# Two graph layers on one core: loads and stores by column of row blocks in place of by partition block, and another order in the front

## The chip, the cores and the metric

One Trainium2 chip, one core of it. The time is that of the device for the whole kernel, in microseconds; the median over runs is compared. A profiled execution gives the trace.

## The reference

32 graphs (batches) of 512 nodes with 512 features each, all float32, through two layers:

```
# layer 0
h   = relu(layernorm(x))
agg = (adj @ h) / max(rowsum(adj), 1e-6)
x   = x + relu(concat(h, agg) @ W.T)               # W: 512 x 1024
# layer 1
h   = relu(layernorm(x))
q, k = split(h @ Wqk);  v = h @ Wv
w   = mask * rowdot(q, adj @ (k * mask)) / sqrt(512)
x   = x + softmax(w over nodes)[:, None] * v
```

## The kernel before

Every 512 x 512 x 512 product is done in float32 on TensorE by a scheme of seven half-size products in place of eight (the tiles named pp, pq, pr hold its sums in PSUM; left and right sums of quadrants are made on DVE). Layer 0 is Y = h W2^T, then o = h W1^T + A Y with A the row-normalized adjacency; layer 1 uses M = Wq Wk^T and computes t = h1 M and v = h1 Wv together (`layer1_tv`, tiles ptv, line 470), u = A (mask h1), and the score as the row product of t and u. So a batch costs TensorE four phases: `layer0_y`, `layer0_out`, `layer1_tv`, `layer1_u`.

A tile of 512 rows holds row q\*128 + c\*32 + r in partition q\*32 + r, column c (q, c from 0 to 3, r from 0 to 31). DVE turns 32 x 32 blocks, so a transposed matrix is made by writing the rows to a scratch in DRAM (dhT, daT, dh1T), reading it back with an exchange of blocks (`exchange`, line 206: four DMAs, one for each q) and turning it on DVE.

The order of all engines is written by hand (`manual_schedule`): each phase is a generator of products, and a `Plan` says after which product the other work is issued. All loads and stores of the steady state are issued on SP's queue, in this order of the program; an issue that has to wait for a semaphore holds everything behind it. x1 is added to the result by an accumulating DMA from POOL (`add_x1`).

The lines that the change and the prediction touch:

- `by_rows` (188), `load_rows` (193), `half_rows` (202): loads of x (tile xu, by `load_x`), of x again for the next batch's layer 0 (tile n, `FrontH.load`), of adj (tile a, `FrontA.load`), and of Wv. Each DMA takes one q: 32 partitions, with 4 columns (256 KB) or 2 (128 KB).
- `store` (714) and, for the last batch, `store_block` (708): the result to DRAM, likewise one DMA for each q.
- w<-dw (line 415): W1's seven slots are streamed from a scratch in DRAM, 256 KB a slot, 128 partitions a DMA, seven per batch.
- `start` (778), the front: it loads Wk in two halves and Wq in four pieces of rows, turns them on DVE, and multiplies them to M on TensorE (`multiply`, line 839) while x[0] arrives, is normalized, and turned through TensorE (h). ACT issues half of these DMAs and does nothing else until its table load at the first copy. Before the data is there, TensorE runs five products of zeros (spare, line 819).

Of the kernel before, what the change touches and what calls it, by code (L numbers as in the profile page):

```python
# [22 lines left out]
def kernel(  # L23
# [11 lines left out]
    nc = tc.nc  # L35
    B, N, F = x.shape
    C = N // P
    H = F // 2
    Q = 4
    R = 32  # L40
# [26 lines left out]
    def mm_tile(name):  # L67
        return ps_m.tile([P, 2, H], F32, tag="m", name=name)
# [10 lines left out]
    def copy(o, i):  # L79
        nc.scalar.activation(o, i, AF.Copy)  # L80
# [104 lines left out]
        def at(self, n, f, *args):  # L185
            self.setdefault(n, []).append(lambda: f(*args))

    def by_rows(src):

        t = src.rearrange("(q c r) f -> q r c f", q=Q, c=C)  # L190
        return [t[q] for q in range(Q)]

    def load_rows(t, src):
        for q, rows in enumerate(by_rows(src)):
            nc.sync.dma_start(out=t[q * R:(q + 1) * R, :, :], in_=rows)

    def half_tile(name):
        return big.tile([P, 2, 512], F32, tag="n", bufs=2, name=name)
# [1 line left out]
    one_queue, two_queues = (nc.sync, nc.sync), (nc.sync, nc.scalar)  # L200

    def half_rows(t, src, h, queues=one_queue):
        for q, rows in enumerate(by_rows(src)):
            queues[q % 2].dma_start(out=t[q * R:(q + 1) * R, :, :], in_=rows[:, 2 * h:2 * h + 2, :])

    def exchange(src, name, t=None, queues=one_queue):


        if t is None:
            t = big.tile([P, 8, P], F32, tag="s", bufs=2, name=name)  # L210
        for q in range(Q):
            queues[q % 2].dma_start(
                out=t[q * R:(q + 1) * R, :, :], in_=src[:, :, ts(q, P)].rearrange("k r j -> r k j")
            )
        return t


    mhalf = const.tile([P, C], F32, name="mhalf")
    nc.vector.memset(mhalf, -0.5)

    X, AT_, DEG, W, Y, H1M, H1T, U, TV, HT = ({} for _ in range(10))

    def xu_tile(name):
        return big.tile([P, C * 512], F32, tag="xu", bufs=2, name=name)

    def room_x(b):

        t = xu_tile(f"xu_{b}")
        X[b] = t.rearrange("p (c f) -> p c f", c=C)
        U[b] = t.rearrange("p (k i f) -> p k i f", k=4, i=2)  # L230

    def load_x(b):
        room_x(b)
        load_rows(X[b], x[b])

    def norm_tiles(name):
        k = name[0]
        mv = small.tile([P, C, 2], F32, tag=f"mv{k}", name=f"mv{name}")
        rstd = small.tile([P, C], F32, tag=f"rstd{k}", name=f"rstd{name}")
        nmr = small.tile([P, C], F32, tag=f"nmr{k}", name=f"nmr{name}")  # L240
        return mv, rstd, nmr

    def statistics(src, t, c, name):
        st = small.tile([P, 6], F32, tag="st", bufs=4, name=f"st{name}_{c}")
        nc.vector.bn_stats(st, src)
        nc.vector.bn_aggr(t[0][:, c, :], st)

    def variance(t, a=0, b=C):
        mv, rstd, nmr = t
        nc.vector.tensor_scalar(rstd[:, a:b], mv[:, a:b, 1], LN_EPS, None, op0=ALU.add)  # L250
        nc.gpsimd.tensor_tensor(rstd[:, a:b], rstd[:, a:b], mhalf[:, a:b], op=ALU.pow)  # L251

    def shift(t, a=0, b=C):
        mv, rstd, nmr = t
        nc.vector.scalar_tensor_tensor(
            nmr[:, a:b], mv[:, a:b, 0], -1.0, rstd[:, a:b], op0=ALU.mult, op1=ALU.mult
        )
# [32 lines left out]
    class FrontH:  # L290
# [8 lines left out]
        def load(self, h, t=None):  # L299
            self.n[h] = half_tile(f"n_{self.b}_{h}") if t is None else t  # L300
            half_rows(self.n[h], x[self.b], h)
# [15 lines left out]
    class FrontA:  # L317
# [9 lines left out]
        def load(self, h):  # L327
            self.n[h] = half_tile(f"a_{self.b}_{h}")
            half_rows(self.n[h], adj[self.b], h)
# [298 lines left out]
    class Post:  # L628
# [77 lines left out]
                )  # L706

        def store_block(self, r, c):
            for q, dst in enumerate(by_rows(out[self.b])):
                (nc.scalar if q % 2 else nc.sync).dma_start(  # L710
                    out=dst[:, 2 * r:2 * r + 2, ts(c, H)], in_=self.o[q * R:(q + 1) * R, 2 * r:2 * r + 2, ts(c, H)]
                )

        def store(self, h):
            v = self.half(h).rearrange("p (c f) -> p c f", c=2)
            for q, dst in enumerate(by_rows(out[self.b])):
                nc.sync.dma_start(out=dst[:, 2 * h:2 * h + 2, :], in_=v[q * R:(q + 1) * R])


    wide = const.tile([P, 14, 2, H], F32, name="wide")  # L720
    w2R, hT = wide[:, 0:7], wide[:, 7:14]
    tv = const.tile([P, 2, 2, 14, P], F32, name="tv")

    def weight_source(src):
        return src.rearrange("(k r) j -> k r j", r=R)

    def turn_right(t, h, k, dst):

        nc.vector.transpose(
            dst[:, 2 * k + h, :, :].rearrange("p b (k r) -> p k b r", r=R),  # L730
            t[:, :, ts(k, 2 * R)].rearrange("p k (c r) -> p k c r", r=R),
        )

    def turn_ordered(t, d, dst):

        nc.vector.transpose(
            dst[:, :, ts(d, P)].rearrange("p a (k r) -> p k a r", r=R),
            t.rearrange("p k (a r) -> p k a r", r=R),
        )

    def turn_natural(t, h, dst):

        nc.vector.transpose(
            dst[:, :, ts(h, H)].rearrange("p a (k r) -> p k a r", r=R),
            t.rearrange("p k (a r) -> p k a r", r=R),
        )

    mraw = const.tile([P, C, B], F32, name="mraw")
# [29 lines left out]
    def start():  # L778

        H1T[0] = big.tile([P, 7, 7, P], F32, tag="h1T", bufs=1, name="late")  # L780
        late = H1T[0].rearrange("p s i f -> p (s i f)")
# [10 lines left out]
        def rows16(n):  # L792
            return room[:, n:n + 2048].rearrange("p (k f) -> p k f", f=P)

        sq, sk, s1 = rows16(0), rows16(2048), rows16(7168)
        wk_rows = weight_source(wqk[:, F:2 * F])
        wq_rows = wqk[:, 0:F].rearrange("(q c r) j -> c q r j", q=Q, c=C)
        exchange(wk_rows[0:8], "swk_0", sk[:, 0:8], two_queues)
        for d in range(C):
            exchange(wq_rows[d], f"swq_{d}", sq[:, 4 * d:4 * d + 4], two_queues)  # L800
        exchange(wk_rows[8:16], "swk_1", sk[:, 8:16], two_queues)
        room_x(0)
        for h in range(2):
            half_rows(X[0][:, 2 * h:2 * h + 2, :], x[0], h, two_queues)
        s2 = []
        for h in range(2):
            s2.append(exchange(weight_source(w0[:, F:2 * F])[8 * h:8 * h + 8], f"sw2_{h}", None, two_queues))
        fa = FA[0] = FrontA(0)
        fa.load(0)
        fa.load(1)  # L810
        exchange(weight_source(w0[:, 0:F]), "sw1", s1)
        fh = FH[1] = FrontH(1)
        wqT = late[:, 0:2048].rearrange("p (c f) -> p c f", c=C)
        wkT = late[:, 2048:4096].rearrange("p (c f) -> p c f", c=C)
        mask_sb, mask_by = late[:B, 4096:4608], late[:B, 4608:5120]

        spare = mm_tile("spare").rearrange("p a f -> p (a f)")
        for n in range(5):
            nc.tensor.matmul(spare, still[:, 0:P], still, start=True, stop=True)

        t = norm_tiles("0_0")
# [5 lines left out]
        v = {}  # L827
# [22 lines left out]
        def place_m(d):  # L850
            place(d, 0, held["m", d].rearrange("p a f -> p (a f)"))

        turn_natural(sk[:, 0:8], 0, wkT)
        for d in range(C):
            turn_ordered(sq[:, 4 * d:4 * d + 4], d, wqT)
        turn_natural(sk[:, 8:16], 1, wkT)
        for h in range(2):
            for c in (2 * h, 2 * h + 1):
                statistics(X[0][:, c, :], t, c, "0_0")
            variance(t, 2 * h, 2 * h + 2)  # L860
            shift(t, 2 * h, 2 * h + 2)
        for h in range(2):
            for k in range(2):
                turn_right(s2[h], h, k, w2R)

        for d in range(C):
            multiply(d, 0)
# [18 lines left out]
        nc.sync.dma_start(out=mask_sb, in_=nodemask)  # L886
        wvN = xu_tile("wvN").rearrange("p (c f) -> p c f", c=C)
        load_rows(wvN, wv)
        r2, l0 = right_sums(of(w2R)), left_sums(of(h0))

        a0 = AT_[0] = slots("aT", 1, "aT_0")
        AT_[1] = a0
        rows = {}
# [7 lines left out]
        p = Plan()  # L901
# [53 lines left out]
        p = Plan()  # L955
# [52 lines left out]
        f = F1[0] = FrontH1(0)  # L1008
# [9 lines left out]
        p = Plan()  # L1018
# [25 lines left out]
        p = Plan()  # L1044
# [22 lines left out]
    }  # L1067
    with tc.manual_schedule(engines=engines):
        weights, mvR = start()
        post = None  # L1070
        for i in range(1, B):
            more, last = i + 1 < B, i + 1 == B
            f = F1[i] = FrontH1(i)
            p = Plan()
# [40 lines left out]
            if 1 < i and i + 2 < B:  # L1115
                fh = FH[i + 2]
                late = i == 2
# [22 lines left out]
            p = Plan()  # L1140
# [53 lines left out]
            p = Plan()  # L1194
# [40 lines left out]
            if more:  # L1235
                p = Plan()
# [25 lines left out]
        p = Plan()  # L1262
# [11 lines left out]
        p = Plan()  # L1274
# [39 lines left out]
```

## Time and profile before

| | |
|---|---|
| median of 3 runs | 2264.93 us (2263.68 to 2269.67) |
| the profiled execution | 2263.74 us |
| its span, first to last instruction | 2262.0 us |
| granted TensorE clock | 1.000 |
| TensorE busy | 2253.7 us (100%) |
| DVE, ACT, POOL busy | 1913.5, 1024.9, 175.6 us |
| moved by DMA | 463.69 MB, 205 GB/s |
| from one batch to the next (rows of line 470 in the chain) | 69.5 us |

A busy time is the sum of an engine's instructions; the chain of waits follows the end of the kernel back to what released each step. A DMA share is the busy share of the core's 16 DMA engines, and a packet is one contiguous run that one DMA engine moves. Times in the profile are microseconds from the first instruction, those of single instructions nanoseconds where marked. All numbers are of one execution.

### The profile page before, as it was taken

Reading aid. Unit: us, or ns where it says so; the run is one execution under the profiler, and the core shown is the slowest. Engines: PE = TensorE matmul, PEld = TensorE weight load, DVE = VectorE, ACT = ScalarE, POOL = GpSimd, SP = SyncE. Lnnn points to the kernel's source line nnn. Section 1 sums busy time; section 2 is a strip of 40 time slices with the busy share of each in tenths; the row PEclk is TensorE's granted clock in tenths of the full one; section 3 lists DMA queues with packets and bytes.
Section 4 is the critical chain, followed back from the end, with each engine's and each line's share of the span. In section 5 each row is a group of like instructions: output and inputs, shape, how many; then the busy total and the mean of one; then the engine's idle time right before and its main releaser. Section 6 shows DMA issues by size and latency. Waiting matters only on the chain.

```text
span 2262.0 us, 32862 instructions
## 1 busy us (share of the span) xinstructions
PE 2253.7 (100%) x10526; PEld 1981.3 (88%) x10526; DVE 1913.5 (85%) x3778; ACT 1024.9 (45%) x1895; POOL 175.6 (8%) x261
## 2 busy tenths in 40 slices
PE   9999999999999999999999999999999999999999
PEld 7888888888888888888888888888888888888888
DVE  7988888888888888888888888888888888888776
ACT  4454443445434544434454344543444443445323
POOL 0010000000000000000000000000000000000000
PEclk9999999999999999999999999999999999999999
DMA  9988787888877887877878788888778777887644
GB/s 205 252 233 246 208 208 193 205 222 219 209 200 192 212 227 204 207 198 201 233 207 209 198 199 218 221 205 203 194 211 228 203 208 193 205 231 209 156 120 108
DMA packets 409997, 463.69 MB, mean 205 GB/s; under 512 B 38208, under 2 KB 271680, under 8 KB 405600
## 3 DMA queue, kind: packets, MB, share of 16 engines
q1 hardware_dynamic: 396608, 426.46, 69.3%
q0 software_dynamic: 8928, 32.51, 8.8%
q10 hardware_dynamic: 4288, 2.62, 0.6%
q8 instruction: 83, 1.36, 0.3%
q14 instruction: 90, 0.74, 0.1%
HBM read 293.93 MB, written 167.51 MB: 204 GB/s over the span
## 4 chain that ended last, share of the span: by engine, by line
PE 98%; DMA 1%; SPq 0%; ACT 0%; issue 0%; DVE 0%; DVEq 0%
PE ptv L470 28%; PE pp_o L103 19%; PE pp_y L103 10%; PE pp_u L103 10%; PE pq_o L103 9%; PE pq_y L103 5%; PE pq_u L103 5%; PE pr_o L103 5%; PE pr_y L103 2%; PE pr_u L103 2%; PE pw L521 1%; DMA mv<-in_L_gnn_Wqk_dram 0%; PE pp_v L103 0%; PE pp_t L103 0%; DMA w<-dw 0%; DMA xu<-in_x_dram 0%
## 5 line engine op out<-in xcount | busy, mean ns | idle before, releaser
L470 PE MATMUL ptv<-mv,h1T 128*128 128x256 f32 x2842 | 618.4, 379 | 0.0
L470 PEld LDWEIGHTS ptv<-mv,h1T 128*128 128x128 f32 x2842 | 539.9, 190 | 73.7 <-DVE xu L449 0.4
L74 DVE TENSOR_TENSOR tv<-tv 128x256 f32<-128x256 f32 (+1 forms) x645 | 322.0, 511 | 13.2 <-ACT tv L80 1.5
L80 ACT ACTIVATE tv<-ptv 128x512 f32<-128x512 f32 (+1 forms) x360 | 185.0, 541 | 262.9 <-PE ptv L470 261.9
L103 PE MATMUL pp_u<-h1m,aT 128*128 128x256 f32 x1024 | 241.9, 379 | 0.0
L103 PE MATMUL pp_y<-wide 128*128 128x256 f32 x992 | 234.4, 379 | 0.7 <-ACT y L80 0.7
L103 PE MATMUL pp_o<-y,aT 128*128 128x256 f32 x992 | 234.3, 379 | 0.0
L103 PE MATMUL pp_o<-w,wide 128*128 128x256 f32 x960 | 226.8, 379 | 0.0
L103 PEld LDWEIGHTS pp_u<-h1m,aT 128*128 128x128 f32 x1024 | 194.5, 190 | 26.4
L103 PEld LDWEIGHTS pp_y<-wide 128*128 128x128 f32 x992 | 188.3, 190 | 26.6 <-ACT y L80 1.1
L103 PEld LDWEIGHTS pp_o<-y,aT 128*128 128x128 f32 x992 | 188.4, 190 | 25.6
L103 PEld LDWEIGHTS pp_o<-w,wide 128*128 128x128 f32 x960 | 182.4, 190 | 24.8
L80 ACT ACTIVATE o<-pp_o 128x512 f32<-128x512 f32 x96 | 57.3, 597 | 300.1 <-PE pp_o L103 300.1
L80 ACT ACTIVATE y<-pp_y 128x512 f32<-128x512 f32 x124 | 74.0, 597 | 234.0 <-PE pp_y L103 234.0
L74 DVE TENSOR_TENSOR tv<-ptv,tv 128x512 f32<-128x512 f32 x240 | 139.9, 615 | 43.2 <-PE ptv L470 39.6
L80 ACT ACTIVATE xu<-pp_u 128x512 f32<-128x512 f32 x127 | 75.8, 597 | 193.6 <-PE pp_u L103 193.6
L77 DVE TENSOR_TENSOR h1T<-h1T 128x512 f32<-128x512 f32 (+1 forms) x183 | 158.3, 879 | 1.2
L251 POOL TENSOR_TENSOR rstd<-rstd,mhalf 128x2 f32<-128x2 f32 (+1 forms) x97 | 79.8, 823 | 642.5 <-DVE rstd L250 642.5
L103 PE MATMUL pq_u<-h1m,aT 128*128 128x256 f32 x512 | 121.0, 379 | 0.0
L74 DVE TENSOR_TENSOR tv<-ptv,m_tv 128x512 f32<-128x512 f32 (+1 forms) x120 | 72.1, 623 | 56.6 <-PE ptv L470 55.4
L103 PE MATMUL pq_y<-wide 128*128 128x256 f32 x496 | 117.3, 379 | 0.0
L103 PE MATMUL pq_o<-y,aT 128*128 128x256 f32 x496 | 117.2, 379 | 0.0
(173 smaller groups left out, 3354.7 us busy)
## 6 DMA issues: line engine op xcount, KB each, us to landing
w<-dw SPq DMA_DIRECT2D x217, 256.0 KB, 4.2
a<-in_adj_dram SPq DMA_DIRECT2D x256, 128.0 KB, 3.0
dx<-xu SPq DMA_DIRECT2D x32, 1024.0 KB, 5.0
sh1T<-dh1T SPq DMA_DIRECT2D x256, 128.0 KB, 3.4
shT<-dhT SPq DMA_DIRECT2D x248, 128.0 KB, 6.0
daT<-a SPq DMA_DIRECT2D x124, 256.0 KB, 3.0
xu<-in_x_dram SPq DMA_DIRECT2D x124, 256.0 KB, 5.4
dh1T<-h1m SPq DMA_DIRECT2D x124, 256.0 KB, 3.2
```

What stands on the lines that cost most here:

```text
L74: (on or nc.vector).tensor_tensor(o, a, b, op=ALU.add)
L77: (on or nc.vector).tensor_tensor(o, a, b, op=ALU.subtract)
L80: nc.scalar.activation(o, i, AF.Copy)
L103: nc.tensor.matmul(p[:, rc, :], lt[:, LEFT[k], dk, ts(rc, P)], right[:, dk, :], start=first and rc == 0 and dk == 0, stop=True, skip_group ...
L251: nc.gpsimd.tensor_tensor(rstd[:, a:b], rstd[:, a:b], mhalf[:, a:b], op=ALU.pow)
L470: nc.tensor.matmul(banks[n][:, :, ts(i, P)], left[:, LEFT[k], LEFT_IN[j], :], mvR[:, RIGHT[k], RIGHT[j], :, :], start=first and i == 0, st ...
L521: nc.tensor.matmul(banks[n][:, ts(i, P)], left[:, LEFT[k], LEFT_IN[j], :], mvR[:, RIGHT[k], RIGHT[j], which, :], start=first and i == 0, s ...
```

## The change

Loads and stores of x, adj, Wv and the result are cut by column in place of by partition block: `by_chunk` gives for each c the rows of all four q, so that one DMA fills all 128 partitions of one column, 256 KB (a half of a tile is two DMAs in place of four). On the DRAM side such a column is four blocks of 32 rows, 64 KB each, 256 KB apart. In the front, Wq's first piece is asked for ahead of Wk's first half; a copy of four values on ACT, which brings the table load, stands behind the first four DMA issues of ACT's queue; Wk's halves are turned in two pieces each; x[0] is loaded on SP's queue alone; the load of W1's rows is cut in two halves of four DMAs; one product of zeros fewer runs; and the statistics of x[0] and the turns of W2 take another order on DVE.

```diff
-    def by_rows(src):
-        t = src.rearrange("(q c r) f -> q r c f", q=Q, c=C)
-        return [t[q] for q in range(Q)]
+    def by_chunk(src):
+        t = src.rearrange("(q c r) f -> c q r f", q=Q, c=C)
+        return [t[c] for c in range(C)]
+
+    def four(v):
+        return v

     def load_rows(t, src):
-        for q, rows in enumerate(by_rows(src)):
-            nc.sync.dma_start(out=t[q * R:(q + 1) * R, :, :], in_=rows)
+        for c, rows in enumerate(by_chunk(src)):
+            nc.sync.dma_start(out=four(t[:, c, :]), in_=rows)
...
     def half_rows(t, src, h, queues=one_queue):
-        for q, rows in enumerate(by_rows(src)):
-            queues[q % 2].dma_start(out=t[q * R:(q + 1) * R, :, :], in_=rows[:, 2 * h:2 * h + 2, :])
+        for c, rows in enumerate(by_chunk(src)[2 * h:2 * h + 2]):
+            queues[c].dma_start(out=four(t[:, c, :]), in_=rows)
...
         def store_block(self, r, c):
-            for q, dst in enumerate(by_rows(out[self.b])):
-                (nc.scalar if q % 2 else nc.sync).dma_start(
-                    out=dst[:, 2 * r:2 * r + 2, ts(c, H)], in_=self.o[q * R:(q + 1) * R, 2 * r:2 * r + 2, ts(c, H)]
+            for a, dst in enumerate(by_chunk(out[self.b])[2 * r:2 * r + 2]):
+                (nc.scalar if a else nc.sync).dma_start(
+                    out=dst[:, :, ts(c, H)], in_=four(self.o[:, 2 * r + a, ts(c, H)])
                 )

         def store(self, h):
             v = self.half(h).rearrange("p (c f) -> p c f", c=2)
-            for q, dst in enumerate(by_rows(out[self.b])):
-                nc.sync.dma_start(out=dst[:, 2 * h:2 * h + 2, :], in_=v[q * R:(q + 1) * R])
+            for c, dst in enumerate(by_chunk(out[self.b])[2 * h:2 * h + 2]):
+                nc.sync.dma_start(out=dst, in_=four(v[:, c, :]))
...
-    def turn_natural(t, h, dst):
+    def turn_natural(t, h, dst, a, b):
         nc.vector.transpose(
-            dst[:, :, ts(h, H)].rearrange("p a (k r) -> p k a r", r=R),
-            t.rearrange("p k (a r) -> p k a r", r=R),
+            dst[:, a:b, ts(h, H)].rearrange("p a (k r) -> p k a r", r=R),
+            t[:, :, a * R:b * R].rearrange("p k (a r) -> p k a r", r=R),
         )
...
+        exchange(wq_rows[0], "swq_0", sq[:, 0:4], two_queues)
         exchange(wk_rows[0:8], "swk_0", sk[:, 0:8], two_queues)
-        for d in range(C):
+        copy(late[:, 5760:5764], mhalf)
+        for d in range(1, C):
             exchange(wq_rows[d], f"swq_{d}", sq[:, 4 * d:4 * d + 4], two_queues)
         exchange(wk_rows[8:16], "swk_1", sk[:, 8:16], two_queues)
-        room_x(0)
-        for h in range(2):
-            half_rows(X[0][:, 2 * h:2 * h + 2, :], x[0], h, two_queues)
+        load_x(0)
...
-        exchange(weight_source(w0[:, 0:F]), "sw1", s1)
+        for h in range(2):
+            exchange(weight_source(w0[:, 0:F])[8 * h:8 * h + 8], f"sw1_{h}", s1[:, 8 * h:8 * h + 8])
...
-        for n in range(5):
+        for n in range(4):
             nc.tensor.matmul(spare, still[:, 0:P], still, start=True, stop=True)
...
-        turn_natural(sk[:, 0:8], 0, wkT)
-        for d in range(C):
+        turn_ordered(sq[:, 0:4], 0, wqT)
+        for a in range(2):
+            turn_natural(sk[:, 0:8], 0, wkT, 2 * a, 2 * a + 2)
+        for d in range(1, C):
             turn_ordered(sq[:, 4 * d:4 * d + 4], d, wqT)
-        turn_natural(sk[:, 8:16], 1, wkT)
+        for a in range(2):
+            turn_natural(sk[:, 8:16], 1, wkT, 2 * a, 2 * a + 2)
```

More of the change, by code (lines that the diff above doesn't have):

```diff
@@ L851, in place_m @@
             place(d, 0, held["m", d].rearrange("p a f -> p (a f)"))
-        turn_natural(sk[:, 0:8], 0, wkT)
-        for d in range(C):
+        turn_ordered(sq[:, 0:4], 0, wqT)
+        for a in range(2):
+            turn_natural(sk[:, 0:8], 0, wkT, 2 * a, 2 * a + 2)
+        for d in range(1, C):
             turn_ordered(sq[:, 4 * d:4 * d + 4], d, wqT)
-        turn_natural(sk[:, 8:16], 1, wkT)
[L857 to L864, printed above, removed]
+        for a in range(2):
+            turn_natural(sk[:, 8:16], 1, wkT, 2 * a, 2 * a + 2)
+        statistics(X[0][:, 0, :], t, 0, "0_0")
+        statistics(X[0][:, 1, :], t, 1, "0_0")
+        variance(t, 0, 2)
+        statistics(X[0][:, 2, :], t, 2, "0_0")
+        shift(t, 0, 2)
+        statistics(X[0][:, 3, :], t, 3, "0_0")
+        variance(t, 2, 4)
+        turn_right(s2[0], 0, 0, w2R)
+        shift(t, 2, 4)
+        turn_right(s2[0], 0, 1, w2R)
+        for k in range(2):
+            turn_right(s2[1], 1, k, w2R)
         for d in range(C):
```

## The prediction

> **What bounds the kernel now.** I read the engine totals and the chain of waits first: is TensorE ever short of work?
>
> ```profile
> PE 2253.7 (100%) x10526; PEld 1981.3 (88%) x10526; DVE 1913.5 (85%) x3778; ACT 1024.9 (45%) x1895; POOL 175.6 (8%) x261
> PE 98%; DMA 1%; SPq 0%; ACT 0%; issue 0%; DVE 0%; DVEq 0%
> ```
>
> It is not: 2253.7 of 2262.0 us are matmul, 8.3 us are not. No rearrangement of loads can win more than these 8.3 us, of which 4.9 lie behind the last matmul. So the question is what the change can lose, and for that I took the next fullest resource, the 16 DMA engines, over one batch in the middle (69.5 us, the repeat of the chain's L470 rows). Windows view (PE, PEld, DVE, ACT, POOL busy, clock, DMA share, GB/s), then the DMA view of that stretch:
>
> ```profile
> 0.00:23.00 23.00, 20.60 (x77) 14.49 (x78) 11.11 (x22) 4.41 (x7) 2.11 (x8) 1.00 0.99 193
> 23.00:45.00 22.00, 21.31 (x111) 18.32 (x110) 17.55 (x33) 13.94 (x29) 0.00 (x0) 1.00 1.10 211
> 1000.00:1069.50 69.50, 69.50 (x323) 61.18 (x322) 59.41 (x119) 31.86 (x59) 5.34 (x8) 1.00 0.79 208
> ```
> ```profile
> q1 hardware_dynamic: 12388, 13.32, 70.0%
> q0 software_dynamic: 288, 1.05, 8.9%
> ...
> out_dram<-tv SPq DMA_DIRECT2D x8, 128.0 KB, 3.1
> ...
> a<-in_adj_dram SPq DMA_DIRECT2D x8, 128.0 KB, 2.9
> ...
> n<-in_x_dram SPq DMA_DIRECT2D x8, 128.0 KB, 3.5
> xu<-in_x_dram SPq DMA_DIRECT2D x4, 256.0 KB, 5.5
> ```
>
> TensorE has no gap, but the DMA engines are 79% busy: 55.0 of 69.5 us each, 14.5 free. The four issue rows that the change reshapes move 8 x 128 KB three times and 4 x 256 KB: 4 MB of the 14.4 MB per batch. In the front (0 to 45 us) the DMA share is already 0.99 to 1.10.
>
> **What a packet costs.** These four transfers move rows of 2 KB: 2048 packets per batch, 128 on each of 16 engines. Two stretches hold almost only such packets; first w<-dw (128 partitions in one DMA), then n and xu (32 partitions in one DMA):
>
> ```profile
> DMA packets 370, 0.68 MB, mean 387 GB/s; under 512 B 39, under 2 KB 39, under 8 KB 370
> q1 hardware_dynamic: 370, 0.68, 105.1%
> ```
> ```profile
> DMA packets 1063, 1.82 MB, mean 243 GB/s; under 512 B 175, under 2 KB 175, under 8 KB 1063
> q1 hardware_dynamic: 1063, 1.82, 100.7%
> ```
>
> The first: 331 packets of 2 KB in 1.051 x 16 x 1.75 us = 29.4 us, 89 ns each. The second: 888 in 1.007 x 16 x 7.5 = 120.8 us, 136 ns each. Shares above 100% say that packet times overlap a little, so both are on the high side.
>
> **The change: the loads and stores.** In the kernel before, a DMA covers one block of 32 partitions, and both of its sides count 32 rows outermost. In the change a DMA covers one column c: 128 partitions on the SBUF side, but on the DRAM side 4 pieces (q) of 32 rows. It removes 12 of the 28 issues per batch on SP's queue (8+8+8+4 become 16; at 0.43 us each, 5 us of SP's time, which is not on the chain, so nothing). What matters is over how many engines such a DMA is spread. The page counts packets by size:
>
> ```profile
> DMA packets 409997, 463.69 MB, mean 205 GB/s; under 512 B 38208, under 2 KB 271680, under 8 KB 405600
> ```
>
> The issue list holds 2388 DMAs, and 38208 / 2388 = 16.0: each leaves 16 small completion packets, one per engine. But every one of them counts 32 rows or more outermost on both sides. No row shows a DMA whose one side has an outermost count of 4, so I bound it: spread over 16 engines as all rows are, or over 4, one for each outermost piece. I take 4, and the same 4 for every such DMA (if they took turns, the price would be near the first rival's): the even sixteenfold split of all 2388 goes with outer counts that are all multiples of 16, and here that count is 4, each piece one run of 64 KB.
>
> [...]
>
> The sum for four engines. Per batch each of 16 engines now spends 128 x 136 ns = 17.4 us on the four transfers and 55.0 - 17.4 = 37.6 us on all else. On four engines, 2048 / 4 = 512 packets each: at 89 ns 45.6 us (the row of 128 partitions, which the new SBUF side has; at 136 ns, the other end, 69.6 us). These four engines then need 37.6 + 45.6 = 83.2 us per batch (107 at the upper price), against 69.5 of TensorE. All other DMAs (w<-dw, the turned tiles, the scratch writes) have a sixteenth of their rows on these four, so all land late, and TensorE waits for w<-dw, for the turned hT, aT and h1T, and for X. The engines' 14.5 us of free time come where SP, whose queue is in order, waits for ACT or PE (L415 waits 10.6 us for PE in this stretch, L347 5.6 us for ACT); a backlog fills most of such holes. I leave about 3 us: 86 us per batch, 16.5 more than now. Full batches are about 29 (the loads end two batches before the end, and the first store comes in the third): 16.5 x 29 = 479 us.
>
> **The change: the front.** Rows of the timeline (start, length):
>
> ```profile
> 7.03 0.71 DVE L736 STREAM_TRANSPOSE late<-mv 128x512 f32<-128x512 f32 x1
> 7.79 6.77 PEld L839 LDWEIGHTS pm<-late 128*128 128x128 f32 x32 [0.71 <-DVE late L736]
> 18.58 1.28 ACT L845 ACT_TABLE_LOAD   x1 [18.58 <-DMA sw<-in_L_gnn_W_dram]
> ```
>
> Asking for Wq's first rows first puts their turn (0.71 us) ahead of Wk's landing, and with Wk turned in two pieces the first product needs 0.7 us behind that landing in place of 2.1; Wk lands some 0.5 us later, behind 256 KB more. Net 0.5 to 1.3 us earlier, and one warm-up product fewer fits that. The 1.28 us table load moves to where ACT holds only DMA issues; it delays the issues behind it on ACT's queue (Wq's other rows, half of Wk) by up to 1.3 us, while that queue today takes 9.0 us for 12 issues of 0.32 us, mostly waiting for landings, so I cost it at nothing (1.3 us if that cover is gone). On DVE a column of x[0] can be read as soon as its own DMA has landed, and the reciprocal roots on POOL run beside the next column's statistics; TensorE's waits for h (0.9) and y (0.7) can shrink by that. The first part of W0 in two halves adds 4 SP issues, 1.7 us, behind adj's loads and ahead of x[1]'s: not on the chain. All of it together: 1 to 3 us won. Against it, on four engines x[0], adj[0], x[1], Wv and adj[1] take 512 / 4 = 128 packets x 89 ns = 11.4 us per MB, one behind the other, in place of 512 / 16 = 32 packets x 136 ns = 4.4 us on sixteen: 5 x 7 = 35 us more on a resource that is full there. TensorE has some slack behind adj[1]; I take 25 us lost (15 to 35). The last stores grow by under 2 us.
>
> Against the profiled execution's 2263.7 us (span 2262.0 plus 1.7 around it; the median shown is 2264.9): 2263.7 + 479 + 25 + 2 = 2770 us. A measurement of this kernel tells about 0.3%, 7 us, from no change.
>
> **Rivals.**
>
> *Spread over sixteen after all.* Then the 2 KB packets fall from 136 to 89 ns, the DMA share per batch from 55.0 to 49.0 us, TensorE stays without gaps at 69.5, and only the front's 1 to 3 us are won: 2261 us, no change by our measure. For it: all 2388 DMAs show sixteen. Against it: none has so short an outer side. The deciding point: 37.6 + 182 / E us for E engines passes 69.5 below E = 5.7; eight engines would cost nothing, four do. [...]
>
> *Four engines, and the holes stay.* If SP's waits keep all 14.5 us free, a batch takes 83.2 + 14.5 = 97.7 us: 28.2 x 29 + 27 more, 3110 us. For it: SP's issues are in order, and a late load makes ACT's writes late, which SP waits for.
>
> *Four engines, packets overlap more.* If the shares overstate (105% and 110% stand in the views) and other packets run faster with twelve engines half idle, a batch may take 73 us: 2263.7 + 3.5 x 29 + 15 = 2380 us. Against it: 387 GB/s in the w stretch, 24 GB/s per engine, is already by far the faster of the two stretches of such packets.
>
> **How the numbers follow.** Four engines with most holes filled: 0.62, between about 2480 and 2950, 2770 as computed. Holes stay: 0.15. Overlap: 0.10. Sixteen: 0.13, of which 0.02 beyond 0.3% faster. So faster 0.02, same 0.11, slower 0.87. The range 2400 to 3150 takes in the likeliest case, most of the second rival (0.13) and half of the third (0.05): 0.80; the upper price of a packet (107 us per batch, about 3380 us) stays outside it, in the 0.20.
>
> **What would show it.** Four engines: the packets under 512 B fall to 25872 (516 reshaped DMAs with 4 completions, 1488 others with 16); sixteen: 32064 (2004 x 16). xu<-in_x_dram lands later than 5.4 us although its DMA covers 128 partitions; w<-dw rises well above 4.2 us; PE shows waits for DMA in every batch; the L470 rows repeat every 80 to 98 us; the mean DMA share falls below 79% although four engines are full. In the front the first product starts near 7 us and the table load stands before 5 us. A span near 2260 with 32064 small packets makes the forecast wrong at its one assumed step; 25872 with a span below 2400 puts the error into the packet price or the overlap.

## The result, and the profile after

The changed kernel takes 2795.4 us (median, 2789.2 to 2802.8) against 2264.2 us before: a ratio of 1.234, 95% interval 1.2318 to 1.2363. The forecast was 2770 us, in a range of 2400 to 3150. The profiled execution's span grew from 2262.0 to 2788.7 us, by 526.7.

The page of the changed kernel, in the order of the prediction: engine totals, chain, packets by size.

```profile
PE 2413.8 (87%) x10524; PEld 2070.5 (74%) x10524; DVE 1914.9 (69%) x3780; ACT 1015.3 (36%) x1896; POOL 176.3 (6%) x261
...
DMA packets 397653, 463.57 MB, mean 166 GB/s; under 512 B 25872, under 2 KB 259344, under 8 KB 393264
...
PE 47%; DMA 38%; ACT 9%; issue 2%; DVE 2%; SPq 1%; ACTq 0%; POOL 0%; DVEq 0%; POOLq 0%
DMA w<-dw 12%; PE pp_o L103 11%; PE pp_u L103 9%; DMA dh1T<-h1m 8%; DMA dhT<-n 8%; PE pp_y L103 8%; DMA a<-in_adj_dram 5%; PE pq_y L103 4%; PE pq_u L103 4%; PE pr_o L103 3%; ACT n L264 2%; PE pr_u L103 2%; ACT tv L80 2%; PE pr_y L103 2%; ACT a L336 2%
```

The same bytes move. The small packets fall from 38208 to exactly the 25872 that were computed for 516 DMAs with four completions each. TensorE, which held 98% of the chain, now holds 47%, and DMAs 38%, foremost w<-dw, dh1T and dhT: transfers whose own shape did not change.

Two DMA views of a batch in the middle; the second is a stretch in which only the column loads of n and xu run, eight in all, issued one behind the other:

```profile
DMA packets 12420, 14.64 MB, mean 169 GB/s; under 512 B 807, under 2 KB 8011, under 8 KB 12286
q1 hardware_dynamic: 12112, 13.47, 50.8%
```
```profile
DMA packets 358, 0.72 MB, mean 102 GB/s; under 512 B 8, under 2 KB 8, under 8 KB 358
q1 hardware_dynamic: 358, 0.72, 26.3%
```

The first covers 1004.5 to 1091.0 us and looks half empty: 59% by all its queues. The second, 1075 to 1082, tells why. With more than one load waiting, the DMA share stands flat at 26.3%, close to 4 of 16, and the rate at 102 GB/s; 350 packets of 2 KB in 0.263 x 16 x 7 us cost 84 ns each.

A flat share alone would also come of a queue that works off one DMA after another, each on four engines of its own. What becomes of a DMA on sixteen engines that is issued behind the columns decides. The write dhT<-n is issued at 1036.05 us, behind two columns of adj (issued at 1034.75 and 1035.39). In the kernel before, the 2388 DMAs leave 38208 small packets (the row "under 512 B"), and their semaphores rise by one as often, 16 times for each DMA; here the second column of adj takes four such steps (7.65 to 8.16 us behind its issue). So I read a step, and a small packet, as one engine that has done its part. First 1037.5 to 1038.5 us, then 1040.5 to 1044:

```profile
DMA packets 115, 0.43 MB, mean 432 GB/s; under 512 B 12, under 2 KB 12, under 8 KB 79
```
```profile
DMA packets 137, 0.31 MB, mean 90 GB/s; under 512 B 8, under 2 KB 8, under 8 KB 129
```

In the first stretch twelve engines finish dhT. In the second the second column's four finish, and only then dhT's last four: by the semaphore, twelve steps 1.95 to 2.09 us behind the issue and four at 7.65 to 8.13. In the kernel before, all sixteen of such a write (issued at 1012.50) come at 1.85 to 2.11. A read shT<-dhT behind the eight columns (issued at 1082.22) has twelve steps by 5.6 us and its last four at 17.8 to 18.6. So DMAs behind the columns do run on the other twelve engines, and behind two columns as behind eight no more than four engines are late: the columns share the same four.

Who waited for whom over the whole run (us in total, times, longest), and then the timeline of TensorE around one such wait:

```profile
ACT h1m L388 <- DMA dh1T<-h1m: 188.4, 29, 7.7
...
PE pp_o L103 <- DMA w<-dw: 172.1, 30, 7.1
ACT a L336 <- DMA a<-in_adj_dram: 165.9, 39, 8.5
...
PE pp_u L103 <- DVE tv L74: 133.7, 29, 5.5
```
```profile
1009.48 1.89 PE L103 MATMUL pq_o<-y,aT 128*128 128x256 f32 x8
1017.24 3.75 PE L103 MATMUL pp_o<-w,wide 128*128 128x256 f32 x8 [5.88 <-DMA w<-dw]
1020.79 2.94 PE L103 MATMUL pp_o<-y,aT 128*128 128x256 f32 x8
1023.56 1.89 PE L103 MATMUL pq_o<-w,wide 128*128 128x256 f32 x8
```

TensorE stands twice per batch. The first time it waits for w: the slot that the product at 1017.24 needs was issued at 1004.51, twelve engines had finished it 8.6 us later, the last four at 11.8 to 12.6. The second time, at pp_u, it waits for DVE, which waits for ACT's masking of h1m (L388); this writes over h1m in place, and so has to wait until the write dh1T has read it. The chain of the same batch (start, us):

```profile
1046.02 7.71 DMA dh1T<-h1m
...
1054.48 0.62 ACT h1m L388
...
1055.13 0.69 DVE h1m L77
1055.82 0.61 DVE tv L74
...
1056.57 3.31 PE pp_u L103 x8
```

Followed back in this way, 28 of the 29 waits of pp_u over 3 us end at dh1T; in the kernel before, ACT waits 0.7 us for dh1T in the whole run. Behind the wait for w eight products take 3.75 and then 2.94 us in place of 1.89: TensorE's clock has fallen (granted 0.94 in this batch, 1.00 before).

### The profile page after: what moved, and what is told of

Its sections match the earlier page's. It is cut to its first block, busy times and chain, and to the rows that moved or that the text cites. A ratio compares the mean times of both kernels' runs of the same rounds, so it can differ in the third digit from the quotient of the medians.

```text
span 2788.7 us, 32128 instructions
## 1 busy us (share of the span) xinstructions
PE 2413.8 (87%) x10524; PEld 2070.5 (74%) x10524; DVE 1914.9 (69%) x3780; ACT 1015.3 (36%) x1896; POOL 176.3 (6%) x261
## 2 busy tenths in 40 slices
DMA packets 397653, 463.57 MB, mean 166 GB/s; under 512 B 25872, under 2 KB 259344, under 8 KB 393264
## 4 chain that ended last, share of the span: by engine, by line
PE 47%; DMA 38%; ACT 9%; issue 2%; DVE 2%; SPq 1%; ACTq 0%; POOL 0%; DVEq 0%; POOLq 0%
DMA w<-dw 12%; PE pp_o L103 11%; PE pp_u L103 9%; DMA dh1T<-h1m 8%; DMA dhT<-n 8%; PE pp_y L103 8%; DMA a<-in_adj_dram 5%; PE pq_y L103 4%; PE pq_u L103 4%; PE pr_o L103 3%; ACT n L264 2%; PE pr_u L103 2%; ACT tv L80 2%; PE pr_y L103 2%; ACT a L336 2%
## 5 line engine op out<-in xcount | busy, mean ns | idle before, releaser
L103 PE MATMUL pp_o<-w,wide 128*128 128x256 f32 x960 | 277.4, 440 | 167.0 <-DMA w<-dw 167.0
L103 PE MATMUL pp_u<-h1m,aT 128*128 128x256 f32 x1024 | 291.4, 436 | 141.2 <-DVE tv L74 133.7
L103 PEld LDWEIGHTS pp_o<-w,wide 128*128 128x128 f32 x960 | 209.5, 222 | 211.2 <-issue 177.4
L103 PEld LDWEIGHTS pp_u<-h1m,aT 128*128 128x128 f32 x1024 | 221.8, 220 | 189.0 <-ACT a L336 143.3
L103 PE MATMUL pp_o<-y,aT 128*128 128x256 f32 x992 | 252.9, 401 | 0.0
L103 PEld LDWEIGHTS pp_o<-y,aT 128*128 128x128 f32 x992 | 206.1, 208 | 34.2
L77 DVE TENSOR_TENSOR h1m<-h1m 128x512 f32<-128x512 f32 x128 | 85.3, 687 | 210.9 <-ACT h1m L388 209.7
L74 DVE TENSOR_TENSOR o<-m_o,o 128x512 f32<-128x512 f32 x32 | 22.2, 692 | 235.2 <-ACT o L80 235.0
L388 ACT ACTIVATE h1m<-h1m,mraw 128x512 f32<-128x512 f32 x124 | 85.0, 710 | 188.4 <-DMA dh1T<-h1m 188.4
L336 ACT ACTIVATE a<-a 128x512 f32<-128x512 f32 x128 | 79.9, 624 | 186.1 <-DMA a<-in_adj_dram 165.9
```

The source lines that it names most:

```text
L74: (on or nc.vector).tensor_tensor(o, a, b, op=ALU.add)
L77: (on or nc.vector).tensor_tensor(o, a, b, op=ALU.subtract)
L103: nc.tensor.matmul(p[:, rc, :], lt[:, LEFT[k], dk, ts(rc, P)], right[:, dk, :], start=first and rc == 0 and dk == 0, stop=True, skip_group ...
L336: nc.scalar.activation(v, v, AF.Copy, accum_out=DEG[self.b][:, c:c + 1])
L388: nc.scalar.activation(self.rows(c), self.raw[c], AF.Copy, scale=mraw[:, c, self.b:self.b + 1])
```

## The experiments

**How much goes over four engines.** The kernel before, with its front, and one, two, three or all of the four transfers by column:

```diff
 # one: the stores;  two: also xu;  three: also n;  loads: also adj, Wv and the last stores
-            for q, dst in enumerate(by_rows(out[self.b])):
-                nc.sync.dma_start(out=dst[:, 2 * h:2 * h + 2, :], in_=v[q * R:(q + 1) * R])
+            for c, dst in enumerate(by_chunk(out[self.b])[2 * h:2 * h + 2]):
+                nc.sync.dma_start(out=dst, in_=v[:, c, :])
```

Expected of the first: 

> The kernel before, with only the result's stores cut by column (1 MB per batch; loads and front as before). Theory 1, the same four DMA engines fill up: they need 37.6 + 3/4 of 17.4 + 512/4 x 89 ns = 62 us per batch, under TensorE's 69.5, so no cost: 2262 to 2275 us, and TensorE still without gaps. Theory 2, every reshaped DMA costs by its own later landing: a quarter of the loss, about 2264 + 130 = 2395 us. Packets under 512 B: 38208 less 124 DMAs x 16 less 124 x 12 = 34736, if only the stores run on four engines.

Of the second: 

> The kernel before, with the result's stores and the load of x into xu cut by column (2 MB per batch). Theory 1: 37.6 + 8.7 + 22.8 = 69.1 us on four engines, the edge: 2264 to 2355 us. Theory 2: half of the loss, about 2530 us.

Of the third: 

> The kernel before, with the stores, xu and the second load of x (n) cut by column (3 MB per batch). Theory 1: 37.6 + 4.4 + 34.2 = 76.2 us plus some 3 us of holes, 9.7 more per batch: about 2545 us. Theory 2: three quarters of the loss, about 2660 us.

Of all: 

> The kernel before with all loads and stores cut by column (also adj and Wv), and the front's order as before. Both theories: nearly all of the loss is here, 2770 to 2820 us; against the full change the front's order shows as a few us at most. If the front's order mattered more, this would lie over 20 us from the full change's 2795.

Measured: 2293.6, 2317.6, 2533.6 and 2792.5 us; ratios 1.0129 (1.0114 to 1.0145), 1.0236 (1.0214 to 1.0257), 1.119 (1.1167 to 1.1212) and 1.2328 (1.2308 to 1.2349). From the first product of the ptv line to that of the last batch (pw) there are 30 batches; the time between, over 30, beside the load on the four engines that the prediction's terms give (2 KB packets at 89 ns):

| by column | load on four engines, us | us per batch |
|---|---|---|
| none | 55.0 | 69.5 |
| stores | 62.1 | 70.3 |
| + xu | 69.1 | 70.8 |
| + n | 76.2 | 77.7 |
| + adj | 83.2 | 85.3 |

The curve bends where the load passes 69.5 us and then follows the load with 1.5 to 2 us on top. A price per DMA, which would have made the steps equal (130 us each), falls: the steps are 29, 24, 216 and 259 us. The full change lies 3 us above all loads alone, and the two intervals overlap, so no part of the loss can be seen that is the front's order.

The first step missed its expectation (2262 to 2275): 29 us although the four engines have room. In the profiled execution 1.3 us of it lie ahead of the first ptv product, 22.4 in the 30 repeats and 5.0 behind the last matmul, where stores by column are still under way. TensorE's gaps in the repeats add up to 22.6 us, all ahead of products of ptv, and the waits of that run say why:

```profile
ACT a L338 <- DMA a<-in_adj_dram: 156.4, 30, 7.6
...
PE ptv L475 <- ACT tv L80: 7.1, 7, 3.2
PE ptv L475 <- ACT m_tv L80: 6.8, 16, 0.5
...
SPq L209 <- DMA dhT<-n: 266.7, 69, 8.4
```

SP holds adj's load until dhT is written (tile n is reused; 112.3 us before, 266.7 here), dhT's rows queue behind the stores, ACT's sum waits for adj, and ACT's copies of ptv stand behind the sum. That is a delay and not a full engine, 0.75 us per batch: the rival theory holds to that size.

**The outer count itself.** The full change with each column in four DMAs of one q (32 partitions, outer count 32), or in two DMAs of two q (64 partitions, outer count 2):

```diff
-            nc.sync.dma_start(out=four(t[:, c, :]), in_=rows)
+            for a in range(0, Q, n):              # n = 1: quarters (there rows[a]), n = 2: pairs; the stores likewise
+                nc.sync.dma_start(out=t[a * R:(a + n) * R, c, :], in_=rows[a:a + n])
```

> The full change, but each column in four DMAs of 32 partitions, 64 KB each: the same columns in the same order and places, one piece of 64 KB per DMA, so 32 rows outermost on both sides. Theory 1 (the outer count of 4 confines a DMA to four engines): the loss goes, 2262 to 2290 us, unless the 48 issues more per batch (0.43 us each, 21 us on SP's queue) cost something themselves; 16 completion packets per DMA. Rival (what costs is the column cut, that is the order in which rows land): it stays near 2795 us.

> The full change, but each column in two DMAs of 64 partitions, 128 KB each, with an outer count of 2 on the DRAM side. Theory 1: two engines carry all of it, 2048 / 2 = 1024 packets x 86 ns = 88 us + 38 = 126 us per batch, plus holes: about 2264 + 59 x 29 = 3975 us (3850 to 4150), 2 completion packets for each reshaped DMA. Rival (four engines whatever the outer count, or a price per DMA): 2750 to 2900 us.

Measured: 2291.0 us (ratio 1.0122, 1.0093 to 1.0151) and 3970.8 us (1.7544, 1.7493 to 1.7595). Packets of the first, then a GB/s row from the second (40 slices of 2.5 us, from 2000 us):

```profile
DMA packets 428635, 463.88 MB, mean 203 GB/s; under 512 B 56832, under 2 KB 290304, under 8 KB 424224
```
```profile
GB/s 51 52 52 47 234 238 50 47 200 195 304 357 154 265 224 48 52 51 50 50 51 57 147 214 121 32 52 51 51 51 121 66 138 266 68 234 43 51 93 105
```

The first leaves 16 completions for each of its 3552 DMAs, and from its third repeat on the ptv line comes every 69.5 us, as before: the columns cost nothing there once no side has an outer count of 4. (The 26 us that its profiled span is longer are 13.6 ahead of the first ptv product, 10 in the first two repeats and 2.4 behind the last matmul. That SP has up to four times as many DMAs to issue for the same bytes is the likely reason; it was not tested.) The second falls to 51 GB/s, half of 102, and the ptv line repeats every 122 to 123 us (2000.75, 2123.51, 2245.97), against 126 computed. That its whole time hit the expected 3975 us within 5 is luck: the repeats are shorter than computed, and the front and the end lose 118 and 32 us that were not in the sum. The outer count is shown as the cause: 16, 4 and 2 engines give 70, 85 and 123 us.

**The clock's part.** The full change, with work for TensorE where it waits for w:

```diff
+        def warm():
+            spare = seed_tile(f"warm_{b}")
+            for n in range(8):
+                nc.tensor.matmul(spare, HT.get(b, hT)[:, 0, 0, 0:P], HT.get(b, hT)[:, 0], start=True, stop=True)
...
+        if warm is not None:
+            warm()
         yield from m(7, pp, False)
```

> The full change, with eight products of 128x512 (0.85 us each at full clock) put ahead of the product that waits for w<-dw in each batch from 2 to 30, into a PSUM tile that nobody reads: TensorE has work while it waits, and its clock need not fall. In the changed kernel that wait is 5.9 us and the products behind it run at half speed for some 5 us, about 2.7 us lost per batch. Theory 1 in its pure form (the four engines set the period): no gain, within 20 us of 2795 us. Rival (the slow clock is a part of the loss on the chain): 2.7 us x 29 = 80 us won, about 2715 us.

Measured: 2764.2 us (1.2213, 1.2177 to 1.2248), 31 us less than the change's median, between the two expectations. In its trace the wait for w is gone and the eight products behind it take 1.89 us; that place costs 2.0 us less per batch (6.86 us of filler where 6.0 us of gap and 2.9 us of slow clock stood). The repeat falls from 85.14 to 84.34 us, 24 us over 30 batches, so more than half of the 2.0 is given back: at this place the slow clock is a small part of the loss. At the second place, pp_u, the products still run slow in this run (3.75 and 2.66 us for eight at 1043.50), and what that costs was not tested.

**The front.** The change's front with loads by partition block, and the same with x[0] in two halves on two queues:

> The change's front alone: Wq's first piece first, Wk turned in pieces, the table load early, x[0] on SP's queue alone, W1 in two halves; all loads and stores by partition block as in the kernel before. Theory of the prediction: 1 to 3 us won, 2261 to 2264 us. Rival: x[0] on one queue in four DMAs that each hold all four columns lands later than in two halves on two queues, which gives the gain back: 2264 to 2268 us.

> The same front, but x[0] in two halves on two queues as in the kernel before. Theory of the prediction: 1 to 3 us won over before, 2261 to 2263 us. If the one-queue load of x[0] is what costs, this is some us faster than the front with it; if not, the two are equal within 1 us.

Measured: 2266.5 us (1.0012, 1.0003 to 1.0021) and 2262.7 us (0.9991, 0.9982 to 1.0000). The rival of the first is right: x[0] on one queue alone makes the front slower than before by 2.4 us. With two queues it is 3.8 us faster than that, and 1.4 us faster than before, a gain whose interval just reaches none. The first statistics of x[0], with one queue and then with two:

```profile
19.19 0.70 DVE L245 BATCH_NORM_STATS2 st<-xu 128x6 f32<-128x512 f32 x1 [3.39 <-DMA xu<-in_x_dram]
16.16 0.69 DVE L245 BATCH_NORM_STATS2 st<-xu 128x6 f32<-128x512 f32 x1 [1.12 <-DMA xu<-in_x_dram]
```

One part of it alone, the early table load in the kernel before:

```diff
         exchange(wk_rows[8:16], "swk_1", sk[:, 8:16], two_queues)
+        copy(late[:, 5760:5764], mhalf)
```

> The kernel before with one thing of the change's front: the copy of four values on ACT, and so the table load, right behind ACT's twelve issues for Wq and Wk. In the kernel before ACT's first copy of M waits 1.28 us for that load while TensorE stands 0.88 us for h. Theory (the table load is the whole gain of the front): 1 to 1.4 us won, 2262.7 to 2263.2 us, h at about 20.2 us in place of 21.2. Rival (the pieces and Wq's order carry it): no change.

Measured: 2263.8 us, ratio 0.9999 (0.999 to 1.0008). h comes at 20.28 us in place of 21.22, as expected, and y's first product at 22.88 in place of 24.15; but the first ptv product stands at 113.87 us (113.57 before). The 1.3 us are given back between the two; this part alone shows no gain.

Last, the five loads of the front that the prediction priced, by partition block, all else as in the change:

> The full change, but x[0], adj[0], x[1], Wv and adj[1], the five loads of the front that the prediction priced, by partition block; all other loads and stores by column. Theory: the changed kernel reaches its first product of line 473 46.8 us later than before (160.35 against 113.57), and that is these five on four engines: it returns to within 5 us of 113.6, and the whole to 2795 - 45 = 2750 us. Rival (loads behind the front, x[1] into xu, x[2], and the slow clock, carry a part): the first product at 120 to 140 us, 2760 to 2780 us.

Measured: 2762.9 us (1.2202, 1.218 to 1.2225), the first ptv product at 134.8 us. The rival is right: of the 46.8 us that the changed front loses, the five loads carry 25.6, and 21.2 stay. Of these, 3.2 are not the columns' at all: the change's front with every load by partition block (the first of the two runs above) reaches that product at 116.74. The 18.0 us from there to 134.8 are left to the other columns and what follows from them, the slow clock included.

## Why the prediction was right, point by point

- **TensorE without gaps, so the change can only lose.** Right: the best front won 1.4 us, if anything, of the 8.3 that were to be had.
- **Four engines, the same four.** This was the one assumed step, a choice of mine between sixteen and four. 25872 packets, the flat 26.3% and the two runs on the outer count show the four; the last four steps of dhT and shT, late behind the columns, show that they are the same. Of outer counts the runs hold three: 32 with 16 completions a DMA (56832 over 3552), 4 with the four engines, and 2 with half of their rate (51 against 102 GB/s).
- **89 ns a packet.** Right: 84 ns on the four engines. The row of 128 partitions was the one to take, not that of 136 ns.
- **86 us per batch.** Measured 85.14 on the mean, 85.3 in the middle of the run. At the measured 84 ns the load on the four engines is 37.6 + 512 x 84 ns = 80.6 us, not 83.2, and the holes are 4.5, not 3: two terms were off by some 2 us each in opposite directions, and that their sum came so close is in part luck. The view below bears out the 37.6: 0.57 of 16 engines over 85 us, less 2048 packets of 84 ns, leaves 38 us per engine.

```profile
1091.00:1176.00 85.00, 73.35 (x320) 63.10 (x319) 58.56 (x118) 31.53 (x59) 4.99 (x8) 0.94 0.57 169
```

  TensorE's own account of the 15.64 us added: about 11.7 of waits and 3.9 of products slowed by the clock (73.35 us busy here against 69.5). The slow clock was not in the prediction; where it was taken away in front of w, the period fell by 0.8 us.
- **Who waits.** w as forecast. The other wait was forecast for turned tiles; it is ACT's, for the write dh1T to have read h1m.
- **29 batches.** There are 30 repeats, 469.1 us more together, in place of 479: the first two take 91.6 and 96.1 us, the last again 69.5.
- **The front, 25 us lost.** Mis-sized: 46.8. The five loads cost 25.6, near the 25 that was taken (35 on the engines, less a slack that was a guess); the change's order of the front costs 3.2. Beyond these, x[1] into xu and x[2] are loaded over the same four engines before the first ptv product too, and I counted full batches only from there on (that these make up the other 18.0, with the slow clock, is read from the order of the program; it was not run).
- **The front's 1 to 3 us won.** Partly wrong. The first product stands at 7.84 us (7.79 before): it needs Wk and Wq's first piece, 768 KB, in whichever order they are asked for, and Wk's first turn starts later (7.07 against 5.69 us), about as much as its turn in pieces wins. x[0] on one queue, which I passed over, costs 3.8 us: with it the front loses 2.4 us, without it it wins 1.4, if anything.
- **The tail, under 2 us.** Mis-sized: 10.8. I looked only at the last block's packets. Behind the last batches 1 MB of stores from tv and 1 MB from out, 128 packets of 2 KB and 256 of 1 KB on each of the four engines, stand one behind the other from 2762.3 us, far longer than the products still to come:

```profile
DMA packets 1568, 2.06 MB, mean 87 GB/s; under 512 B 48, under 2 KB 1072, under 8 KB 1568
q1 hardware_dynamic: 1040, 1.54, 17.9%
q10 hardware_dynamic: 528, 0.52, 6.4%
```

  (2765.0 to 2788.7 us: 24.3% of 16 engines over the whole stretch, four of them full.)
- **The rivals.** Sixteen engines is out. Of the other two, holes that stay gave 97.7 us per batch and packets that overlap more gave 73; the measured 85 lies between them.

The sum, span against span: 469.1 + 46.8 + 10.8 = 526.7, as measured; predicted 479 + 25 + 2 = 506.

## What to carry to other kernels

Before a transfer is given another shape, read the outermost count of both of its sides, not only its partitions: a count of 4 confined a 128-partition DMA to four engines, and a mean DMA share of 58% then hid four that were busy for some 95% of a batch (80.6 of 85.1 us, an estimate from the terms above). Count the completion packets (small packets over DMAs): 16.0 each before, 12.9 after (25872 over 2004); the fall below 16 came from the columns, and with these in quarters it was 16.0 again (56832 over 3552). And sum the load on the busiest engines against the period of the engine that sets the time; up to that point the cost was 24 to 29 us a step, beyond it over 200.

## What the runs showed of the hardware

A column DMA on four engines took SP about 0.57 us to issue, the shortest 0.53; one on sixteen in the kernel before took about 0.43, the shortest 0.31 (SP's rows for n and the stores). So fewer DMAs saved less of SP's time than counted. Whether the four engines or the longer pattern on the DRAM side cost this was not tested.

Waits of 4.7 and 5.9 us were enough for TensorE's clock to fall to half (granted 0.50 from 1017.24 to 1022.00 us, behind the 5.9), and it took 4 to 6 us of products to come back (behind the 5.9: 3.75 and 2.94 us for eight, then 1.89; behind the 4.7: 3.31 and 2.28). A wait of 3.2 us in the run with the stores alone (at 200.05 us) left the products behind it at full rate (14 in 3.29 us and 28 in 6.31, then eight in 1.89). Work put into the wait kept the clock up (eight products behind it in 1.89 us), but gained only 0.8 us per batch.
